# Layers 1 and 2 of a codebook convolution block: table products of units 0 and 1 issued two units sooner, and a new order of the loads ahead of the second layer

## The chip, the cores and the metric

The kernel runs on one core of one Trainium2 chip. The metric is the device time of the whole program in microseconds (us). The core has five engines, each of which executes its own queue in order: PE (matrix products; its weight loads are shown apart as PEld), DVE (vector), ACT (activations), POOL (general) and SP, which here only issues transfers. An engine whose next instruction waits for another engine lets everything behind that instruction wait too.

## The reference, cut to what matters

The input is `x`, 32 images of 1024 channels and 14 x 14 places. The first block replaces three convolutions by table look-ups with a softmax, and the second block is a linear attention, which this change does not touch.

```python
def _amm(patches, centroids, lut, inv_temp):
    ...
    v = patches.reshape(B, ncb, sub, H * W).transpose(0, 3, 1, 2)
    scores = 2.0 * jnp.einsum('blcs,cks->blck', v, centroids) - jnp.sum(centroids * centroids, -1)[None, None]
    attn = jax.nn.softmax(scores * inv_temp, axis=-1)
    out = jnp.einsum('blck,cko->blo', attn, lut)
    return out.transpose(0, 2, 1).reshape(B, -1, H, W)
...
out = _amm(x, c1_centroids, c1_lut, c1_invt)                      # layer 1
out = jax.nn.relu(_bn(out, bn1_g, bn1_b))
out = _amm(_extract3x3(out, 1), c2_centroids, c2_lut, c2_invt)    # layer 2
out = jax.nn.relu(_bn(out, bn2_g, bn2_b))
out = _amm(out, c3_centroids, c3_lut, c3_invt)                    # layer 3
out = _bn(out, bn3_g, bn3_b)
return jax.nn.relu(out + identity)
```

`_bn` normalises over the whole batch, so layer 2 can't begin before layer 1 has ended, and layer 3 not before layer 2. The input of the block is `_gn(x)`, a group normalisation for each image.

## The kernel before, in words

Four stages follow one another: layer 1, layer 2, layer 3, and the attention. Layers 1 and 2 are driven by the same function `units` (L732). The work of a layer is cut into 128 units: 16 pairs of images, and for each pair eight blocks b of 512 table rows. One unit is

- scores: small matmuls into four PSUM banks (`score1`, L903; `score2`, L1035), and four exponentials on ACT that empty them into one of six tiles `t` (L576);
- the softmax: DVE transposes `t` (L588), adds up groups of 16 (L607), inverts (L609) and transposes the inverses back (L619); POOL multiplies them onto `t` (L626), for every fourth unit with a part set aside as "spare" (L621). From unit 2 on, POOL first adds the halves of the transposed tile (L591), so DVE adds up half as much. The program's order is kept: `units` issues the transpose of unit u one turn before the rest of its softmax;
- `spare_rows` (L717): SP copies rows of the spare into `t`, one transfer or, for every fourth unit, three;
- the table product `lut(u)` (L739): 6 or 8 matmuls, recorded as 12 or 16, into two PSUM banks "po", which are held for the eight units of a pair.

Turn i of `units` issues, in this order: the scores and exponentials of unit i + 4, the transpose of unit i + 3, the softmax of an earlier unit (unit 0 in turn -3, unit 1 in turn -2, then unit 2 in turn 0, unit 3 in turn 1 and so on) with its spare rows, side work `side(i)`, and last `lut(i)` from turn 0 on.

The side work of the first turns includes the preparation of the tables, once per block b and layer, in `packed_lut` (L679): `less` subtracts the last row of each group with two matmuls and two ACT copies (L700, L701), `keep` stores a part of the table to memory (only b = 0 and 4, L704), and `others` loads it back into the block's free rows (L707). `lut(b)` needs all of it for its block. `less` writes to the "po" banks (three of them), or, for b above 5, to the "sc" banks of the scores (four of them). Layer 1 places this work by a list of turns (L857). In layer 2 the first four blocks come before `units`, and `side2` (L1054) has the others. Turns 0 to 2 of layer 1 also carry the group normalisation of the second pair: two matmuls (L274) and small DVE operations (L282 to L288).

Layer 2 reads 3 x 3 neighbourhoods. ACT writes one half (128 channels) of a pair of images into a padded tile (`store_pair`, L987), three transfers bring it to memory as `h1d`, and six transfers per unit (`load_patches`, L1005) bring the shifted rows into one of four patch tiles. All these are issued by SP, except where `engines=both` gives every second one to ACT's queue. Units 0 to 3 of a pair need half 0, units 4 to 7 half 1.

Of the kernel before, what the change touches and what calls it, by code (L numbers as in the profile page):

```python
# [149 lines left out]
def conv_preact_kernel(ctx: ExitStack, tc: tile.TileContext, a: dict, out: bass.AP):  # L150
# [356 lines left out]
    def layers(exact, early=None):  # L507
# [38 lines left out]
        def tap_row(dy, dx):  # L546
            return 8 * dx + dy if dx < 2 else 3 + dy
# [16 lines left out]
        def scores(n):  # L564
            return ps_sc.tile([P, 512], F32, tag="sc", name="sc")[:, :n]
# [7 lines left out]
        def exponentials(t, scs, bias):  # L573

            for j, sc in enumerate(scs):
                nc.scalar.activation(  # L576
                    t[:, j, : sc.shape[1]],
                    sc,
                    AF.Identity if exact else AF.Exp,
                    bias=bias[:, j : j + 1],  # L580
                )

        def token_major(pool, t, two=False, halve=False):


            tf = t.rearrange("p j n -> p (j n)")
            tt = pool.tile([P, tf.shape[1]], F32, tag="tt", name="tt", bufs=2 if two else 1)
            nc.vector.transpose(tt, tf)  # L588
            tv = tt.rearrange("p (m k) -> p m k", k=KC)
            if halve and not exact:  # L590
                nc.gpsimd.tensor_tensor(tv[:, :, :8], tv[:, :, :8], tv[:, :, 8:], ALU.add)  # L591
                tv = tv[:, :, :8]
            return tt, tv
# [85 lines left out]
        def packed_lut(layer, b):  # L679


            v = weights[b].rearrange("p (s w) -> p s w", s=4)
            kept = tables[2 * layer - 2 + b // 4].rearrange("(c k) w -> c k w", k=KC)
            j0 = 0 if b % 4 else 1
            k0 = b % 4 - 1 if b % 4 else 3

            def own():
                if layer == 1:
                    nc.sync.dma_start(v, lut1_tiles[b].rearrange("j c k w -> (c k) j w"))
                    return  # L690
                for c in range(4):
                    nc.sync.dma_start(v[32 * c : 32 * c + 32], lut2_tiles[b, c])

            def less():
                for h in range(2):
                    t = weights[b][:, 512 * h : 512 * h + 512]
                    ps = scores(512) if b > 5 else None
                    if ps is None:
                        ps = ps_po.tile([P, 512], F32, tag="po", name="less")
                    nc.tensor.matmul(ps, less_last, t, start=True, stop=True)  # L700
                    nc.scalar.copy(t, ps)  # L701

            def keep():
                nc.sync.dma_start(tables[2 * layer - 2 + b // 4], v[:, 0])  # L704

            def others():
                nc.sync.dma_start(v[15::16, j0:], kept[:, k0 : k0 + 13 - 4 * j0 : 4])  # L707

            return v, own, less, keep, others


# [20 lines left out]
        def units(ahead, ts, pool, luts, score, bias, dst, stats, side, last, halve=False):  # L732

            n = 8 * NP
            po, late, tts = [], [], {}

            def lut(u):  # L739
                p, b = divmod(u, 8)  # L740
                if b == 0:
                    po[:] = [
                        ps_po.tile([P, 512], F32, tag="po", name="po")[:, :N2] for h in range(2)
                    ]
                j0 = 0 if b % 4 else 1
                order = [(h, j) for h in range(2) for j in range(j0, 4)]
                for h, j in order if b == 7 else sorted(order, key=lambda k: k[1]):
                    nc.tensor.matmul(  # L748
                        po[h],
                        luts[b][:, j, h * P : (h + 1) * P],  # L750
                        ts[u % len(ts)][:, j, :N2],
                        start=(b == 0 and j == j0),
                        stop=(b == 7 and j == 3),
                    )
                if b == 7:
                    for h in range(2):
                        o = dst[:, h, p * N2 : (p + 1) * N2]
                        nc.scalar.copy(o, po[h])
                        late.append((stats[:, h, p, :], o))

            for i in range(-ahead, n):
                u = i + ahead
                if u < n:
                    scs = score(u)
                    exponentials(ts[u % len(ts)], scs, bias[:, 4 * (u % 8) :][:, :4])
                u = i + ahead - 1
                if 0 <= u < n:
                    tts[u] = token_major(pool, ts[u % len(ts)], halve, halve and u >= DIRECT)
                if halve and u >= DIRECT:
                    u = u - 1 if u > DIRECT else n  # L770
                if 0 <= u < n:
                    softmax(
                        pool,
                        u,
                        ts[u % len(ts)],
                        *tts.pop(u),
                        spare=spares[u // 4 % 2] if u % 4 == 0 else None,
                        steps=(1, 1, 1) if u == 0 and not exact else None,
                    )
                    spare_rows(ts, u)  # L780
                while late:
                    nc.vector.bn_stats(*late.pop(0))
                side(i)
                if i >= 0:
                    lut(i)
            for h in range(2):
                nc.vector.bn_stats(*late.pop(0))
                last(h)
# [4 lines left out]
        with ExitStack() as s:  # L793
# [11 lines left out]
            def at(i, piece):  # L805
                todo.setdefault(max(i, -AHEAD - 1), []).append(piece)
# [30 lines left out]
            def side(i):  # L837
                for f in todo.pop(i, []):
                    f()
# [10 lines left out]
            luts2 = [packed_lut(2, b) for b in range(8)]  # L850
# [3 lines left out]
                    at(8 * p + c - AHEAD - 1 - (p == 0), normalise(p, c))  # L854
            at(24, edges)
            at(40, masks2)
            for b, i in enumerate((-4, -3, -3, -2, -2, -1, -1, 0)):  # L857
                for k in (2, 3, 4):
                    if k != 3 or b % 4 == 0:
                        at(i, lambda b=b, k=k: luts[b][k]())  # L860
# [110 lines left out]
        with ExitStack() as s:  # L971
# [15 lines left out]
            def store_pair(p, h, engines=(nc.sync,)):  # L987
                t = pads[h]
                nc.scalar.activation(
                    t.rearrange("p (i r c) -> p i r c", r=15, c=15)[:, :, :14, :14],  # L990
                    out1[:, h, p * N2 : (p + 1) * N2].rearrange(
                        "p (i r c) -> p i r c", r=14, c=14
                    ),
                    AF.Relu,
                    bias=bi1[:, h : h + 1],
                    scale=sc1[:, h : h + 1],
                )
                for x in range(3):
                    c0 = LEAD + 2 * p * IMG + 1 - x
                    v = h1d[x // 2][h, :, :, c0 : c0 + 2 * IMG]  # L1000
                    engines[x % len(engines)].dma_start(v[:, x::2] if x < 2 else v, t)
# [3 lines left out]
            def load_patches(u, engines=(nc.sync,)):  # L1005
                p, b = divmod(u, 8)
                h, g = divmod(b, 4)
                for n, (src, rows) in enumerate(zip(h1d, (8, 16))):
                    for dy in range(3):
                        c0 = LEAD + 2 * p * IMG + 15 * (dy - 1)  # L1010
                        engines[dy % len(engines)].dma_start(
                            pbuf[u % NPB][tap_row(dy, 2 * n) :: rows, :, :SPAN],
                            src[h, 4 * g : 4 * g + 4, :, c0 : c0 + SPAN].rearrange(
                                "q r n -> r q n"
                            ),
                        )

            both = nc.sync, nc.scalar
            store_pair(0, 0, engines=both)
            luts2[0][2]()  # L1020
            luts2[1][2]()
            load_patches(0, engines=both)
            load_patches(1)
            luts2[0][3]()
            luts2[2][2]()
            luts2[3][2]()
            store_pair(0, 1)
            load_patches(2)
            luts2[7][1]()
            for b in range(4):  # L1030
                luts2[b][4]()
            load_patches(3)
            w9, bias2 = parts[2]

            def score2(u):  # L1035
# [16 lines left out]
            ahead = 1 if exact else 4  # L1052
# [429 lines left out]
    engines = {ENG.PE, ENG.DVE, ENG.Activation, ENG.Pool, ENG.SP}  # L1482
    pre = ctx.enter_context(ExitStack())
    early, weights4, repeated = attention_inputs(pre)
    with tc.manual_schedule(engines=engines):
        again = layers(False, early)
# [800 lines left out]
```

## Time and profile before

| | |
|---|---|
| median of three runs | 3363.78 us (3362.78 to 3363.94) |
| profiled execution, its own time | 3366.47 us |
| its span | 3364.7 us, mean granted PE clock 0.993 |
| layer 1, from its first matmul to the end of its last table product | about 10 to 828 us |
| layer 2, the same | about 838 to 1637 us |
| PE busy over the span | 98% |
| DVE, POOL, ACT busy over the span | 85%, 75%, 53% |

The busy shares are averages over four stages with different limits. The change concerns the first 100 us of layer 1 and the first 90 us of layer 2. A timeline entry reads: start, duration, engine, line, operation, output and input, number of merged instructions, and in brackets how long the engine had been idle and what ended it.

### The profile page before, as it was taken

How to read it: one execution, taken by the hardware profiler on the slowest of the kernel's cores; microseconds unless marked ns; L12 is line 12 of the kernel's file. 1: busy time of each engine (PE TensorE's matmuls, PEld its weight loads, DVE VectorE, ACT ScalarE, POOL GpSimd, SP SyncE). 2: the span in 40 equal slices, each digit the busy share in tenths (PEclk: the TensorE clock that was granted, in tenths of full speed). 3: DMA queues.
4: the chain of work that ended last, by engine and by line, in shares of the span. 5: the costliest groups of instructions: out<-in, count | busy, mean ns of one | idle time of the engine just before them, and what ended most of it. 6: DMA issues, size and time to landing. Idle time of an engine off the chain costs nothing. (4 is left out here: it accounts for less than half of the span.)

```text
span 3364.7 us, 61037 instructions
## 1 busy us (share of the span) xinstructions
PE 3300.0 (98%) x22287; PEld 2014.9 (60%) x22287; DVE 2871.1 (85%) x4174; ACT 1788.2 (53%) x4419; POOL 2528.3 (75%) x1562
## 2 busy tenths in 40 slices
PE   8999999999899999999999999998999999999999
PEld 4555555554344444454478888885666666666665
DVE  8999999997788899888656667655899999999996
ACT  4555555554444444444311111107888888888886
POOL 5999999997788888888432222215988888888888
PEclk9999999999999999999999999999999999999999
DMA  3110110102444344443231111113233333232321
GB/s 120 46 49 28 47 47 28 46 28 73 143 124 124 110 123 126 119 115 109 64 81 50 50 50 41 47 47 125 66 89 98 90 89 98 78 91 84 94 81 49
DMA packets 242253, 266.34 MB, mean 79 GB/s; under 512 B 32812, under 2 KB 239700, under 8 KB 241944
## 3 DMA queue, kind: packets, MB, share of 16 engines
q1 hardware_dynamic: 241104, 261.79, 26.6%
q8 instruction: 180, 2.95, 0.4%
q14 instruction: 129, 1.06, 0.1%
q10 hardware_dynamic: 840, 0.55, 0.1%
HBM read 171.01 MB, written 75.58 MB: 73 GB/s over the span
## 5 line engine op out<-in xcount | busy, mean ns | idle before, releaser
L626 POOL TENSOR_TENSOR t<-t,r 128x1568 f32<-128x1568 f32 (+5 forms) x292 | 962.1, 3296 | 535.3 <-issue 223.8
L748 PE MATMUL po<-t,lut 128*128 128x392 f32 x3840 | 1329.5, 499 | 5.8 <-DMA t<-spare 4.8
L748 PEld LDWEIGHTS po<-t,lut 128*128 128x128 f32 x3840 | 709.3, 190 | 602.2 <-issue 71.0
L1794 PE MATMUL mm<-y,lut 128*128 128x392 f32 x2048 | 714.6, 494 | 1.8 <-DVE k L1810 1.8
L588 DVE STREAM_TRANSPOSE tt<-t 128x1568 f32<-128x1568 f32 (+1 forms) x284 | 517.7, 1823 | 155.9 <-ACT t L576 152.8
L576 ACT ACTIVATE t<-sc,cbias 128x392 f32<-128x392 f32 (+1 forms) x624 | 322.4, 598 | 560.8 <-PE sc L909 188.4
L2018 DVE SCALAR_TENSOR_TENSOR pa<-y,lepe_w,pa 128x406 f32<-128x406 f32 x900 | 536.7, 638 | 19.3 <-PE pa L2000 17.0
L619 DVE STREAM_TRANSPOSE r<-rc 128x1568 f32<-128x1568 f32 (+1 forms) x284 | 520.8, 1834 | 11.6 <-POOL t L626 1.2
L1794 PEld LDWEIGHTS mm<-y,lut 128*128 128x128 f32 x2048 | 369.4, 188 | 243.5 <-issue 6.3
L591 POOL TENSOR_TENSOR tt<-tt 128x784 f32<-128x784 f32 x252 | 463.5, 1839 | 11.2 <-DVE tt L588 11.1
L576 ACT ACTIVATE t<-sc,room 128x392 f32<-128x392 f32 x512 | 259.1, 589 | 392.2 <-issue 162.9
L1376 PE MATMUL po<-t,lut 128*128 128x224 f32 (+2 forms) x1352 | 315.0, 416 | 0.0
L607 DVE TENSOR_REDUCE sm<-tt 128x98 f32<-128x784 f32 (+2 forms) x284 | 297.0, 1046 | 1.6 <-POOL tt L591 0.8
L1376 PEld LDWEIGHTS po<-t,lut 128*128 128x128 f32 (+1 forms) x1352 | 234.6, 190 | 63.2 <-issue 60.6
L609 DVE RECIPROCAL rc<-sm 128x98 f32<-128x98 f32 (+1 forms) x284 | 220.2, 775 | 9.8
L630 ACT ACTIVATE sm<-sm 128x98 f32<-128x98 f32 (+1 forms) x284 | 85.3, 300 | 157.0 <-DVE rc L609 157.0
L1980 POOL TENSOR_TENSOR qr<-qr,zb 128x784 f32<-128x784 f32 x64 | 118.3, 1856 | 49.4 <-DMA zb<-zd 49.2
L1647 ACT ACTIVATE w<-x,tb,gn_a 128x196 f32<-128x196 f32 x248 | 128.3, 517 | 35.9 <-POOL y L1529 28.4
L1806 ACT ACTIVATE e<-e 128x392 f32<-128x392 f32 x256 | 134.4, 525 | 1.0
L1043 PE MATMUL sc<-patch,room 27*32 27x392 f32 x4096 | 124.0, 509 | 8.6 <-DMA patch<-h1d 6.6
L1760 ACT ACTIVATE y<-x,gb,ga 128x196 f32<-128x196 f32 x256 | 123.3, 541 | 13.6 <-POOL gb L1723 13.6
L1389 DVE TENSOR_TENSOR o<-po,o 128x224 f32<-128x224 f32 (+1 forms) x156 | 81.6, 543 | 56.7 <-PE po L1376 51.9
(215 smaller groups left out, 4523.1 us busy)
## 6 DMA issues: line engine op xcount, KB each, us to landing
patch<-h1d SPq DMA_DIRECT2D x383, 108.5 KB
x<-in_x_dram SPq DMA_DIRECT2D x32, 784.0 KB
o3d<-o SPq DMA_DIRECT2D x56, 448.0 KB
x<-in_x_dram SPq DMA_DIRECT2D x64, 392.0 KB
out_dram<-x SPq DMA_DIRECT2D x64, 392.0 KB
o<-o3d SPq DMA_DIRECT2D x62, 392.0 KB
h1d<-pad SPq DMA_DIRECT2D x95, 225.0 KB
patch<-h1d SPq DMA_DIRECT2D x383, 54.2 KB
```

Of the source, the lines that this page charges most:

```text
L576: nc.scalar.activation(t[:, j, : sc.shape[1]], sc, AF.Identity if exact else AF.Exp, bias=bias[:, j : j + 1],)
L588: nc.vector.transpose(tt, tf)
L591: nc.gpsimd.tensor_tensor(tv[:, :, :8], tv[:, :, :8], tv[:, :, 8:], ALU.add)
L607: nc.vector.tensor_reduce(sm, tv, AX.X, ALU.add)
L609: nc.vector.reciprocal(rc, sm)
L619: nc.vector.transpose(r, bc(rc, 2, KC))
L626: nc.gpsimd.tensor_tensor(v[:, c], v[:, c], r[:, c], ALU.mult)
L748: nc.tensor.matmul(po[h], luts[b][:, j, h * P : (h + 1) * P], ts[u % len(ts)][:, j, :N2], start=(b == 0 and j == j0), stop=(b == 7 and j = ...
L1376: nc.tensor.matmul(dst, w, x, start=start, stop=stop)
L1794: nc.tensor.matmul(pv(), w[kt][:, m0 : m0 + P], ywin(p, first + kt), start=(kt == 0), stop=(kt == 3),)
L1806: nc.scalar.activation(e(), e(), AF.Exp, scale=-1.0)
L2018: nc.vector.scalar_tensor_tensor(acc, neighbours(p, c, offset(k)), lw[:, c, k : k + 1], acc, ALU.mult, ALU.add,)
```

## The change

The diff does five things.

1. `units`: `lut(0)` is issued at the end of turn -2 and `lut(1)` at the end of turn -1. Turns 0 and 1 issue no table product, and from turn 2 on all is as before. This holds for layers 1 and 2.
2. `less` of blocks 4 and 5 writes to the "sc" banks as well.
3. The preparation of the tables of layer 1 is spread differently: by blocks 0 to 7, turns -4, -4, -3, -3, -1, 0, 0, 1 instead of -4, -3, -3, -2, -2, -1, -1, 0.
4. The first `store_pair` of layer 2 is issued by SP alone. The patches of unit 1 are issued by SP and ACT in turn.
5. Ahead of layer 2's `units`, the patches of units 2 and 3 come before the store of half 1, the load-back of block 0 (`others`) comes between them, and the raw table of block 7 is loaded last.

```diff
@@ -694,7 +694,7 @@
-                    ps = scores(512) if b > 5 else None
+                    ps = scores(512) if b > 3 else None
...
@@ -781,8 +781,9 @@
                 side(i)
-                if i >= 0:
-                    lut(i)
+                k = {-2: 0, -1: 1, 0: -1, 1: -1}.get(i, i) if ahead > 2 else i
+                if k >= 0:
+                    lut(k)
...
@@ -854,7 +855,7 @@
-            for b, i in enumerate((-4, -3, -3, -2, -2, -1, -1, 0)):
+            for b, i in enumerate((-4, -4, -3, -3, -1, 0, 0, 1)):
                 for k in (2, 3, 4):
                     if k != 3 or b % 4 == 0:
                         at(i, lambda b=b, k=k: luts[b][k]())
...
@@ -1016,20 +1017,21 @@
             both = nc.sync, nc.scalar
-            store_pair(0, 0, engines=both)
+            store_pair(0, 0)
             luts2[0][2]()
             luts2[1][2]()
             load_patches(0, engines=both)
-            load_patches(1)
+            load_patches(1, engines=both)
             luts2[0][3]()
             luts2[2][2]()
             luts2[3][2]()
+            load_patches(2)
+            luts2[0][4]()
+            load_patches(3)
             store_pair(0, 1)
-            load_patches(2)
+            for b in range(1, 4):
+                luts2[b][4]()
             luts2[7][1]()
-            for b in range(4):
-                luts2[b][4]()
-            load_patches(3)
             w9, bias2 = parts[2]
```

Here `luts[b][1]` to `luts[b][4]` are `own` (the raw load), `less`, `keep` and `others` of block b.

## The prediction

> **What bounds the kernel now.** I read the page's slices first, then engine busy time by windows, then the timelines of the two places where the slices show gaps, and last SP's own waits.
>
> ```profile
> PE   8999999999899999999999999998999999999999
> DVE  8999999997788899888656667655899999999996
> ```
>
> A slice is 84 us. PE has a gap only at the start, where layer 1 turns into layer 2, and later where the attention begins. Windows (PE, PEld, DVE, ACT, POOL busy, then PE clock):
>
> ```profile
> 20.00:40.00 20.00, 15.62 (x49) 6.55 (x48) 16.21 (x24) 14.37 (x33) 6.66 (x8) 0.85 0.37 119
> 40.00:60.00 20.00, 20.00 (x73) 9.76 (x73) 18.76 (x30) 13.30 (x31) 16.28 (x7) 1.00 0.35 101
> 600.00:800.00 200.00, 200.00 (x776) 104.03 (x776) 188.28 (x203) 108.06 (x272) 187.95 (x84) 1.00 0.09 27
> 850.00:870.00 20.00, 14.44 (x85) 5.42 (x86) 14.56 (x11) 9.69 (x22) 13.26 (x8) 0.77 0.54 160
> ```
>
> In the steady part PE is full, and DVE and POOL are at 94%. So a delay at the start stays to the end of a layer if it is PE's. One of DVE is made good slowly, about 1.7 us per eight units. PE is idle for 4.4 us between 20 and 40 and not at all from 40 on: there is hardly a hole in which the early products could go. Layer 1's timeline:
>
> ```profile
> 33.72 2.53 SPq L728 DMA_DIRECT2D t<-spare  x3
> 40.83 0.94 PE L909 MATMUL sc<-x,cw 32*128 32x392 f32 x8
> 43.50 0.60 SPq L725 DMA_DIRECT2D t<-spare  x1
> 49.90 0.20 DVE L282 TENSOR_TENSOR gd<-gst,gn_ps 128x32 f32<-128x32 f32 x1 [0.75 <-PE gn_ps L274]
> 50.67 1.80 DVE L588 STREAM_TRANSPOSE tt<-t 128x1568 f32<-128x1568 f32 x1
> 71.03 3.52 POOL L626 TENSOR_TENSOR t<-t,r 128x1568 f32<-128x1568 f32 x1
> 79.65 5.51 PE L748 MATMUL po<-t,lut 128*128 128x392 f32 x16
> ```
>
> These are the spare rows of units 0 and 1, the scores of unit 3, DVE's wait for the group means, the transpose of unit 4, and unit 5's last multiplication and table product. Layer 2:
>
> ```profile
> 857.05 1.62 PE L1043 MATMUL sc<-patch,room 27*32 27x392 f32 x32 [4.07 <-DMA patch<-h1d]
> 858.75 1.98 SPq L728 DMA_DIRECT2D t<-spare  x3
> 876.71 0.62 SPq L725 DMA_DIRECT2D t<-spare  x1
> 879.07 5.50 PE L748 MATMUL po<-t,lut 128*128 128x392 f32 x16 [0.69 <-DMA t<-spare]
> 905.07 5.50 PE L748 MATMUL po<-t,lut 128*128 128x392 f32 x16 [1.93 <-DMA t<-spare]
> ```
>
> ```profile
> SPq L1001 <- DMA h1d<-pad: 2.4, 1, 2.4
> ```
>
> PE waits for patches, then twice for spare rows (units 2 and 6). Unit 2's were multiplied by 869.83 (POOL, 866.29 + 3.54) but issued at 876.71: SP, busy almost without a break with 0.62 us per patch transfer, is the limit there.
>
> **What the Trainium skill says.** "TensorE: Matmul & The Clock Gate", Part 1, What's actually happening: after about 3.4 us without work the clock is halved, and about 3.4 us of work bring it back. The trace agrees: after PE's pause from 853 to 857 the windows show 0.50 until 862. "DMA: Bandwidth & Descriptors", Issuing engines are not separate DMA queues: a second issuing engine saves issue time only. Here SP's third store waits 2.4 us for another store, which the split brought with it. Same page, Two DMAs through the same engine are not ordered: a dependent transfer must wait for completion. The trace prices that: 876.71 to 879.07, 2.35 us from issue to use.
>
> **Layer 1, step by step.**
> 1. Unit 0's tile is multiplied by 35.66 and its third spare transfer issues at 35.68; with 2.35 it is ready at 38.0. Turn -2 leaves PE nothing after unit 2's scores (about 34.3), so PE waits 3.7 us in front of `lut(0)`, with unit 3's scores behind it. 12 records take 4.2 us: 42.2. Such a wait can also halve the clock; then 43.9.
> 2. Unit 3's scores then go at 42.2 instead of 40.83, its exponentials end 0.96 + 2.02 later, at 45.2. DVE is free at 43.6: it stalls 1.6 us where it stalled 0.26.
> 3. `lut(1)` waits for unit 1's spare row, 43.50 + 2.35 = 45.85 (block 4's `less` fits ahead of it), and takes 5.5: 51.35. Behind it stand unit 4's scores (before: 45.33). Exponentials end at 54.3.
> 4. Behind those now stand `less` of blocks 5 and 6, in score banks that the exponentials must free first: 52.8 to 56.3 (four at 0.86). Then the group-mean matmuls, 0.7. DVE's group-norm step goes at 57.2 instead of 49.90, and with 0.8 for it unit 4's transpose at 58.0 instead of 50.67: 7.3 us late.
> 5. From there to unit 5's tile the trace shows DVE idle 0.4 us and POOL following it, so 74.55 becomes about 81.9, ready at 84.25. Unit 5's product ran at 79.65 and was ready at 74.57 + 2.35 = 76.9: slack 2.75. It starts 4.6 late, 5.9 with the halved clock. I take 5.2.
> 6. Later units have their slack (unit 12: 0.7 us, but DVE has 2 us of idle time ahead of it), so 0 to 0.5 more, taken as 0.
>
> The four `less` copies taken out of turns -2 and -1 save ACT time that only shortens its own idleness. They cost nothing early because unit 1's and 2's exponentials (30.6, 36.5) still precede DVE's need (33.5, 40.8). Bank choice costs what step 4 holds.
>
> **Layer 2.**
> 1. SP's queue. The wait of 2.4 goes, 0.45 for one more store comes, two patch issues (1.23) go to ACT, and a 0.5 wait mostly goes. The rest is reordered: I count 41 issues from 829.4 and reach unit 0's spare rows at 854.8 instead of 858.75. ACT gains two issues (0.6 to 1.4 each) ahead of the copies of blocks 2 and 3, for which block 3's `less` and the first scores wait; it loses one store issue. First scores: -0.45, bounds -1.2 to +0.5. Block 7's raw table lands before 853 and is needed past 870: nothing.
> 2. Patches of unit 3 land at about 848 instead of 857. But `lut(0)` now stands before unit 3's scores: spare rows 854.8, third issue 856.1, landed 858.4. PE has then idled since about 852.4, so half clock for its first 3.5 us: ends 864.3. Unit 3's scores go 7.2 us later than before, its transpose at 867.35 instead of 860.84.
> 3. `lut(1)` 867.5 to 873.0 (two `less` ahead of it); unit 4's scores 873.0 instead of 862.83; its transpose 876.05 instead of 866.66. So 9.4 late.
> 4. Unit 2's multiplication ends at 876.3; its spare row issues at 876.35 instead of 876.71, since SP had been late. SP now waits 4 us for it, and again for unit 3's (884.9 instead of 881.85): 3.1 late. From there SP is as full as before, and unit 6's product starts about 3.2 later than 905.07. After that PE is full. I take +3.1. At full clock in step 2 it is 1.4; with an extra ACT delay and a slower unit 5, 4.5.
>
> Both layers end in a batch norm, so the two add: 5.2 + 3.1 = +8.3. Profiled: 3366.47 + 8.3 = 3374.8. The median of the runs is 2.7 lower than the profiled time: 3363.78 + 8.3 = 3372.1. About 0.2% (6.7 us) is what a measurement can tell from no change.
>
> **Rivals.**
> - Layer 2 pays for layer 1: SP's saved 3.2 us reach unit 6's product because SP never waits for DVE. Then +5.2 - 3.2 = +2: 3366. For it: that product waits on a spare row. Against: DVE's 9.4 is larger than the 6.9 of SP's lateness at unit 2.
> - Nothing moves by more than a us or two, since slack at unit 5 swallows most: 3364. Against: 7.3 is far over 2.75.
> - Faster: DVE does not starve, because the reordered exponentials reach it in time. Its stalls of 1.4 between 40 and 67 and the 2.75 of slack go in layer 1, 3.2 in layer 2: -7.3, 3356.5. The place is unit 4's transpose in layer 1, and it decides if that starts before 50.67 + 2.75 = 53.4. For it: DVE, not PE, bounds units 2 to 5. Against: `lut(1)` can't end before 51.35.
>
> **How the numbers follow.** Both layers delayed 0.64 (its own range +4 to +12, a fifth of it under 6.7), layer 2 pays 0.15, nothing 0.07, faster 0.14. Slower 0.50, same 0.14 + 0.15 + 0.07 = 0.36, faster 0.14. Range: up to +13 (3377), down to -3 (3361), which leaves out the faster case and little else.
>
> **What would show it.** Right: in layer 1 `lut(0)` near 38 after a PE wait for a spare row, unit 4's transpose near 58, unit 5's product near 84 with a wait before it; in layer 2 unit 3's scores behind `lut(0)` near 864, and SP waiting for POOL at units 2 and 3. Wrong: unit 4's transpose before 54, or DVE without a gap between 50 and 57; or layer 2's unit 6 earlier, counted from the end of layer 1.

## The result, and the profile after

| | before | after |
|---|---|---|
| median of six runs | 3363.86 us (3362.64 to 3364.93) | 3393.95 us (3392.75 to 3396.72) |
| ratio, 95% interval | | 1.0091 (1.0078 to 1.0104) |
| profiled execution, its own time | 3366.47 us | 3393.07 us |
| its span | 3364.7 us | 3390.4 us |

The kernel is slower by 30.1 us, where the prediction had 8.3. The sign was right, the size was not. The page of the kernel after, slices (part 2) and one group (part 5, which ends in the idle time ahead of the group and what ended most of it), then the same group of before:

```profile
PE   7999999999899999999999999999999999999998
DVE  7999999997788898888666666655899999989996
...
L748 PE MATMUL po<-t,lut 128*128 128x392 f32 x3840 | 1334.5, 500 | 13.3 <-DMA t<-spare 7.4
```

```profile
L748 PE MATMUL po<-t,lut 128*128 128x392 f32 x3840 | 1329.5, 499 | 5.8 <-DMA t<-spare 4.8
```

The table products wait 13.3 us in all (before: 5.8), so they can't hold 30. PE's first slice fell from 8 to 7, as a loss in layer 1's first turns would have it, but its last slice fell too, from 9 to 8, and that lies in the attention, in which no line was changed. The span cut at four places of the trace says how much each stage took. Layer 1 ends here at the first copy that empties its last product, layer 2 at layer 3's first `less` matmul, layer 3 at the attention's first transposing matmul:

| us | layer 1 | layer 2 | layer 3 | attention |
|---|---|---|---|---|
| before | 825.5 | 811.4 | 647.7 | 1080.1 |
| after | 831.7 | 816.3 | 646.0 | 1096.5 |
| difference | +6.2 | +4.9 | -1.7 | +16.4 |

(The -1.7 is not the change's: layer 3 took either 645.7 to 646.0 or 647.4 to 647.7 in every profile of this study, though its code is the same in all.) These are two single executions: their differences add up to 25.7 us, where the medians differ by 30.1, and a stage with unchanged code repeats to within some 2 us. The two layers together lost 11.1, not far from the forecast. More than half of the loss is where the prediction had no term at all.

First the layers. Layer 1 after, timeline entries of SP, PE and DVE:

```profile
33.70 2.52 SPq L728 DMA_DIRECT2D t<-spare  x3
35.61 4.19 PE L748 MATMUL po<-t,lut 128*128 128x392 f32 x12 [1.31 <-DMA t<-spare]
45.73 7.20 PE L748 MATMUL po<-t,lut 128*128 128x392 f32 x16 [2.42 <-POOL tt L591]
52.86 0.94 PE L910 MATMUL sc<-x,cw 32*128 32x392 f32 x8
58.55 0.20 DVE L282 TENSOR_TENSOR gd<-gst,gn_ps 128x32 f32<-128x32 f32 x1 [9.66 <-PE gn_ps L274]
59.31 1.80 DVE L588 STREAM_TRANSPOSE tt<-t 128x1568 f32<-128x1568 f32 x1
64.64 1.40 PE L910 MATMUL sc<-x,cw 32*128 32x392 f32 x4 [1.41 <-ACT lut L701]
65.97 7.23 PE L748 MATMUL po<-t,lut 128*128 128x392 f32 x16
85.82 5.51 PE L748 MATMUL po<-t,lut 128*128 128x392 f32 x16
```

`lut(0)` and `lut(1)` stand at 35.61 and 45.73, each behind a wait. (The view puts the second down to POOL; it fits unit 1's spare row, issued at 43.48, as well.) Unit 4's scores come behind the second, then DVE stands still for 9.66 us in front of the group means, and unit 4's transpose starts at 59.31 instead of 50.67. The products of units 1 and 2 took 7.2 us instead of 5.5 (the granted clock was 0.83 from 40 to 50 and 0.85 from 60 to 70, where before had 1.00), and unit 5's starts 6.2 late. Layer 2 after:

```profile
862.86 1.98 SPq L728 DMA_DIRECT2D t<-spare  x3
864.95 5.88 PE L748 MATMUL po<-t,lut 128*128 128x392 f32 x12 [2.44 <-issue]
873.90 1.81 DVE L588 STREAM_TRANSPOSE tt<-t 128x1568 f32<-128x1568 f32 x1 [11.84 <-ACT t L576]
882.81 1.81 DVE L588 STREAM_TRANSPOSE tt<-t 128x1568 f32<-128x1568 f32 x1 [3.59 <-ACT t L576]
882.90 0.62 SPq L725 DMA_DIRECT2D t<-spare  x1
915.25 5.50 PE L748 MATMUL po<-t,lut 128*128 128x392 f32 x16 [2.68 <-DMA t<-spare]
```

These times hold layer 1's 6.2. Without it unit 0's spare rows are issued at 856.7, `lut(0)` starts at 858.8, the transposes of units 3 and 4 start at 867.7 and 876.6, unit 2's spare row is issued at 876.7 and unit 6's product starts at 909.1, that is 4.0 later than the 905.07 of before.

Now the attention. Windows over its whole length (busy time of PE first, then PEld, DVE, ACT, POOL), of before and of after:

```profile
2284.60:3364.70 1080.10, 1062.48 (x10102) 690.10 (x10102) 976.41 (x2062) 902.74 (x2230) 938.86 (x862) 0.99 0.30 87
```

```profile
2293.90:3390.40 1096.50, 1064.07 (x10102) 689.82 (x10102) 977.87 (x2062) 904.07 (x2230) 939.64 (x863) 0.99 0.29 86
```

The same work by the same counts of instructions (one more on POOL), but PE idles 32.4 us instead of 17.6. So the order differs. It shows best at two small DVE operations for each of the 16 pairs of images, the means `kmm` (L1926 before, L1928 after), for which the normaliser's matmuls wait. Timeline of before, for pair 2 and pair 16:

```profile
2393.42 0.18 DVE L1926 TENSOR_TENSOR kmm<-ks,hmean 128x32 f32<-128x32 f32 x1
2394.06 1.20 DVE L1926 TENSOR_TENSOR kmm<-ks,hmean 128x32 f32<-128x32 f32 x1
2415.35 1.53 PE L1944 MATMUL mm<-q,kmm 128*32 128x196 f32 x32 [0.39 <-DVE q L1810]
...
3300.68 1.82 DVE L1926 TENSOR_TENSOR kmm<-ks,hmean 128x32 f32<-128x32 f32 x2
3320.59 1.53 PE L1944 MATMUL mm<-q,kmm 128*32 128x196 f32 x32
```

And of after, with two of POOL's entries beside the last:

```profile
2401.64 0.18 DVE L1928 TENSOR_TENSOR kmm<-ks,hmean 128x32 f32<-128x32 f32 x1
2435.92 0.19 DVE L1928 TENSOR_TENSOR kmm<-ks,hmean 128x32 f32<-128x32 f32 x1
2436.76 1.51 PE L1946 MATMUL mm<-q,kmm 128*32 128x196 f32 x32
...
3350.66 1.71 POOL L1840 TENSOR_TENSOR qr<-q,cosq 128x784 f32<-128x784 f32 x1
3352.99 8.02 DVE L1928 TENSOR_TENSOR kmm<-ks,hmean 128x32 f32<-128x32 f32 x2
3358.86 7.36 POOL L2057 TENSOR_TENSOR x<-x,side 128x392 f32<-128x392 f32 x7
3363.18 1.53 PE L1946 MATMUL mm<-q,kmm 128*32 128x196 f32 x32
```

Before, the two means of pair 2 are 0.6 us apart and 22 us ahead of the normaliser. After, the second is 34 us behind the first, directly ahead of the normaliser. For the last pair both hang beside POOL's unbroken run, and the normaliser comes 1069.2 us after the start of the attention instead of 1036.0, with 27 us to the end.

Why should an untouched stage be ordered otherwise? Its order is not written out. A planner (`Plan`, L51) writes it from pieces with ranks. The lines that matter are L90 and L127:

```python
engines = {p[0] for p in self.pieces}
...
for e in engines:
    ...
    if locked and any(t > now for o, t in port.items() if o != e):
        rest.append((r, n))
        continue
```

`engines` is a set of strings. The order in which Python walks such a set is drawn anew in every build. Pieces marked `port=True` hold a lock that DVE and POOL share in the plan: nearly all of these are POOL's, and the means are DVE's only ones. Where POOL is asked first, it takes the lock again the moment it is free, and the means get in only once POOL has nothing ready. The planner's loop, run off the chip over all 120 orders of the five engines, gives just two plans, one for DVE ahead of POOL and one for POOL ahead of DVE, 60 orders each, for before and after alike. By the planner's own clock, which adds up the durations written beside the pieces, the first ends at 1084.8 us and the second at 1102.7. Theory: before was built with the first, after with the second, and the 19 us that the layers leave of the 30.1 have nothing to do with the diff. Rival: the diff reaches the attention through the state in which it leaves the engines, buffers or queues, or the layers' delay shifts it.

### The profile page after: what moved, and what is told of

It reads as the page before. It is cut to its first block, busy times and chain, and to the rows that moved or that the text cites. A ratio compares the mean times of both kernels' runs of the same rounds, so it can differ in the third digit from the quotient of the medians.

```text
span 3390.4 us, 61032 instructions
## 1 busy us (share of the span) xinstructions
PE 3303.7 (97%) x22287; PEld 2015.7 (59%) x22287; DVE 2871.6 (85%) x4174; ACT 1790.1 (53%) x4419; POOL 2528.6 (75%) x1562
## 5 line engine op out<-in xcount | busy, mean ns | idle before, releaser
L748 PE MATMUL po<-t,lut 128*128 128x392 f32 x3840 | 1334.5, 500 | 13.3 <-DMA t<-spare 7.4
L2020 DVE SCALAR_TENSOR_TENSOR pa<-y,lepe_w,pa 128x406 f32<-128x406 f32 x900 | 534.5, 638 | 22.2 <-PE pa L2002 19.9
L591 POOL TENSOR_TENSOR tt<-tt 128x784 f32<-128x784 f32 x252 | 463.4, 1839 | 29.9 <-DVE tt L588 29.8
L609 DVE RECIPROCAL rc<-sm 128x98 f32<-128x98 f32 (+1 forms) x284 | 220.2, 775 | 9.8
L630 ACT ACTIVATE sm<-sm 128x98 f32<-128x98 f32 (+1 forms) x284 | 85.1, 300 | 160.4 <-DVE rc L609 160.3
L825 ACT ACTIVATE x<-x,gn_b,gn_a 128x196 f32<-128x196 f32 x256 | 127.6, 557 | 5.1 <-POOL gn_b L296 3.4
```

What stands on the lines that cost most here:

```text
L609: nc.vector.reciprocal(rc, sm)
L748: nc.tensor.matmul(po[h], luts[b][:, j, h * P : (h + 1) * P], ts[u % len(ts)][:, j, :N2], start=(b == 0 and j == j0), stop=(b == 7 and j = ...
L2020: nc.vector.scalar_tensor_tensor(acc, neighbours(p, c, offset(k)), lw[:, c, k : k + 1], acc, ALU.mult, ALU.add,)
```

## Experiments: the attention

The runs below were made in three batches, each beside the kernel before and on the same chip as it. Its medians there were 3363.36, 3363.97 and 3364.00 us for runs 1 to 4, 5 to 8 and 9 to 12: the build with DVE first, as run 1 will show.

**1. The kernel before, with POOL first.**

```diff
-        engines = {p[0] for p in self.pieces}
+        engines = ["PE", "POOL", "ACT", "DVE", "SP"]
```

> The kernel before with one line changed: the planner of the attention goes through its engines in a written order with POOL ahead of DVE, instead of in the order of a Python set of strings. Theory 'plan' (the attention's order of instructions depends on the set's order, which the build draws anew, and the changed kernel drew the other one): the attention takes about 1096.5 us instead of 1080.1, total +16, near 3380. Rival 'carried over' (layers 1 and 2 leave something behind that slows the attention): no difference, 3364.

Measured: 3381.73 us (3379.57 to 3384.29), ratio 1.0057 (1.0044 to 1.0071), +18.4. Timeline entries of it:

```profile
2388.98 0.18 DVE L1926 TENSOR_TENSOR kmm<-ks,hmean 128x32 f32<-128x32 f32 x1
2423.28 0.19 DVE L1926 TENSOR_TENSOR kmm<-ks,hmean 128x32 f32<-128x32 f32 x1
2424.11 1.51 PE L1944 MATMUL mm<-q,kmm 128*32 128x196 f32 x32
...
3340.22 8.03 DVE L1926 TENSOR_TENSOR kmm<-ks,hmean 128x32 f32<-128x32 f32 x2
```

The same gap of 34 us and the same 8 us at the end as in after, without a line of the change.

**2. The kernel after, with DVE first** (the list `["PE", "DVE", "ACT", "POOL", "SP"]` in the same place, as in all the runs that follow but number 11).

> The changed kernel with the same line written with DVE ahead of POOL. Theory 'plan': the attention is back at 1080, total near 3363.9 + 9.4 = 3373 to 3377; what is left are about 6 us of layer 1 and 4 to 5 of layer 2. Rival 'carried over': still near 3394.

Measured: 3374.83 us (3372.73 to 3379.35), ratio 1.0037 (1.0025 to 1.0050), +11.5. 11.5 and 18.4 add up to 29.9, which is the result's 30.1 within their intervals (each some 4 us to either side). The start of the normaliser's matmuls, in us from the start of the attention, is the fingerprint:

| pair | 1 | 2 | 3 | 15 | 16 |
|---|---|---|---|---|---|
| before | 68.1 | 130.8 | 195.7 | 974.7 | 1036.0 |
| run 2, the change with DVE first | 68.1 | 130.8 | 195.7 | 974.6 | 1036.0 |
| after | 67.0 | 142.8 | 196.4 | 988.7 | 1069.2 |
| run 1, before with POOL first | 68.2 | 144.0 | 197.4 | 989.7 | 1070.3 |
| run 11 (below) | 67.6 | 131.1 | 195.3 | 982.2 | 1045.3 |

The attention follows the order of the engines in the planner, and not the change: the rival falls. (The attention as a whole took 1096.5 and 1097.5 us in after and run 1, and 1080.1 and 1080.5 in before and run 2.)

**11. POOL first, but the means don't ask for the lock.**

```diff
-                do(DVE, rank - 10, 0.2, means(i), allk, [("kmm", i)], port=True)
+                do(DVE, rank - 10, 0.2, means(i), allk, [("kmm", i)])
```

> The kernel before with GpSimd named ahead of VectorE in the planner of the attention stage, as in the run that cost 18.4 us, but with the two small means of each pair no longer asking for the shared lock. Theory A, that the lock alone makes the order matter, by holding back these means: 0 to 4 us above before. Theory B, that GpSimd's own order of pieces makes the loss: 14 to 19 us above before.

Measured: 3376.13 us (3372.62 to 3377.72), ratio 1.0034 (1.0022 to 1.0047), +12.1: between the two theories. Pair 2 is back at 131.1, and the hole ahead of the last pair is gone. With this edit the two orders of the engines give the very same instructions in the same order on every engine, so it is through the lock at the means, and only there, that the order acts. But leaving the lock out is no cure. All instructions of this tile (number, then shortest, median and longest in ns), in before and in run 11:

```profile
L1926 DVE TENSOR_TENSOR kmm<-ks,hmean x32: 175/209/1757, 2329.6 to 3300.8; 128x32 f32<-128x32 f32 x32
```

```profile
L1926 DVE TENSOR_TENSOR kmm<-ks,hmean x32: 175/828/1757, 2327.6 to 3307.0; 128x32 f32<-128x32 f32 x32
```

Planned without the lock, the means run beside POOL's operations and last four times as long in the median. The Trainium skill has a reason ("SBUF — State Buffer", SBUF: two separate sides): a DVE operation with two SBUF inputs and a GpSimd (POOL) operation that reads SBUF need the same port pair, which one takes for a whole instruction while the other is blocked. The trace agrees as to these means: 0.18 us alone, 8.0 us for two beside POOL's run in after. DVE's busy time in the attention is 986.3 us here against 976.4 in before. How the 12 us split between such blocking and the other plan that comes of it was not settled; the planner's own clock, which leaves blocking out, ends this plan at 1083.1 us, no later than before's.

## Experiments: the two layers

**3 and 4. Each layer's share alone.** The turn of `lut` and the banks made to depend on the layer; run 3 has layer 1's new products, banks and spread and layer 2 as before, run 4 the reverse (with the new loads).

```diff
-                k = {-2: 0, -1: 1, 0: -1, 1: -1}.get(i, i) if ahead > 2 else i
+                k = {-2: 0, -1: 1, 0: -1, 1: -1}.get(i, i) if ahead > 2 and soon else i
```

> DVE ahead of POOL in the planner; layer 1 as changed (products sooner, weights later, blocks 4 and 5 in score banks), layer 2 as before. My theory (DVE starved by the early products): +6.2 over the kernel before, unit 5's product of layer 1 near 85.8. Rival (the two layers' costs do not add, a late layer 1 is made good later): under +3.

> DVE ahead of POOL in the planner; layer 2 as changed (products sooner, new order of loads), layer 1 as before. My theory: +4 to +5 over the kernel before, unit 6's product of layer 2 about 4 later, counted from the end of layer 1. Rival (the loads pay for the products): 0 or below.

Measured: layer 1 alone 3370.15 (3366.99 to 3375.05), ratio 1.0019 (1.0012 to 1.0027), +6.8; layer 2 alone 3369.19 (3364.33 to 3372.86), ratio 1.0015 (1.0008 to 1.0022), +5.8. Their sum, 12.6, is run 2's 11.5 within the intervals: they do add. The traces agree. Layer 1, counted from its first scores because these start anywhere from 19.9 to 22.1 us, took 809.5 to 809.9 us in the three traces with all of its change (after, runs 2 and 3), and 803.3 to 803.8 in the eight with its old code. Layer 2 took 814.9 to 818.6 where it was changed (after, runs 2, 4 and 8), and 809.3 to 811.4 in the five with its old code. Run 3's trace has unit 5's product at 85.5, run 4's has unit 6's 83.7 us behind the end of layer 1 (before 79.6, after 83.6).

**12. Everything but the two products**, which stay in turns 0 and 1 in both layers (the line of runs 3 and 4, with `soon` never set).

> The whole change with VectorE named first, except that the table products of units 0 and 1 keep their old place in both layers. Theory A, that their sooner place makes the layers' loss: what is left is the later table preparation of layer 1 (1.9 us measured alone) and the new loads (1.0 us the other way), so 0 to 3 us above before. Theory B, that the table preparation and the score banks lent to unit 4's and 5's tables carry half of it: 5 us or more above before.

Measured: 3365.67 (3362.51 to 3372.30), ratio 1.0006 (0.9997 to 1.0014), +1.7. By the medians some 10 of run 2's 11.5 go with the place of these two products, but the interval of 1.7 alone reaches from -1 to +5, and the trace says so for layer 2 only. Layer 2 took 809.7 there, as with its old code. Layer 1, counted from its first scores, took 807.5: still 3.7 to 4.2 more than the old code, with the products in their old place. PE and DVE in turns -1 and 0:

```profile
39.38 2.93 PE L700 MATMUL sc<-lut,less_last 128*128 128x512 f32 x3 [2.45 <-ACT t L576]
45.44 5.36 PE L700 MATMUL sc<-lut,less_last 128*128 128x512 f32 x8
51.19 0.20 DVE L282 TENSOR_TENSOR gd<-gst,gn_ps 128x32 f32<-128x32 f32 x1 [2.69 <-PE gn_ps L274]
```

PE waits 2.45 us for score banks in front of block 4's weight difference, works at half clock behind that (0.50 from 40 to 48, where before had 1.00), and DVE waits 2.69 for the group means. So, by this one trace, the table preparation and its banks delay layer 1 by themselves, and only some 2 of its 6 us go with the products. How far the parts depend on each other was not settled: no run has layer 1's new products with the old spread and banks.

**7. Layer 1's spread of the table preparation alone.**

```diff
-            for b, i in enumerate((-4, -3, -3, -2, -2, -1, -1, 0)):
+            for b, i in enumerate((-4, -4, -3, -3, -1, 0, 0, 1)):
```

> The kernel before (DVE ahead of POOL) with only the new turns of the table preparation of layer 1, and the products where they were. My theory (the early products are what costs): within 1.5 of the kernel before. Rival (blocks 5 and 6 moved in front of the group means are what costs): +3 or more.

Measured: 3365.86 (3361.40 to 3372.52), ratio 1.0007 (1.0001 to 1.0014), +1.9. A small cost, between the theories; in the trace layer 1, from its first scores, is 2.1 to 2.6 longer than with the old code (805.9). Its timeline shows where:

```profile
48.59 5.05 PE L748 MATMUL po<-t,lut 128*128 128x392 f32 x10 [2.07 <-ACT lut L701]
...
57.54 0.17 DVE L288 TENSOR_SCALAR gve<-gn_ps 128x16 f32<-128x16 f32 x1 [3.03 <-PE gn_ps L274]
```

Within unit 0's product PE now waits 2.07 us for ACT's copies of a weight difference that is made in the same turn, in the "po" banks that the product needs. DVE waits 3.03 for the second group mean, which stands on PE behind the next block's weight difference.

**8. The change with DVE first, and the first two group-mean steps one turn sooner**, so that they stand ahead of `lut(1)`.

```diff
-(-3, -3, -2, -1, 0, 0, 1, 1, 2)[k]
+(-3, -3, -2, -1, -1, 0, 1, 1, 2)[k]
```

> The changed kernel (DVE ahead of POOL) with one piece moved: the group-mean matmuls of layer 1 are issued a turn sooner, ahead of the product of unit 1. My step 4 (3.4 us of DVE's stall are the wait for these matmuls behind four weight matmuls, the rest is unit 4's exponentials): DVE's transpose of unit 4 near 55.9 instead of 59.3, total 3.4 below the changed kernel with this planner order, near 3371.5. Rival (PE itself, not DVE, sets the end of the ramp): unchanged, 3375.

Measured: 3371.82 (3371.26 to 3375.11), ratio 1.0026 (1.0014 to 1.0037): 3.0 below run 2, near the 3.4 of the forecast. The two intervals overlap; in the traces layer 1 from its first scores is 2.3 shorter than in run 2 (807.2 and 809.5).

```profile
48.66 0.15 DVE L282 TENSOR_TENSOR gd<-gst,gn_ps 128x32 f32<-128x32 f32 x1
...
55.73 1.81 DVE L588 STREAM_TRANSPOSE tt<-t 128x1568 f32<-128x1568 f32 x1 [6.27 <-ACT t L576]
...
63.93 5.53 PE L748 MATMUL po<-t,lut 128*128 128x392 f32 x16
```

The group means are done at 48.66, and unit 4's transpose, 3.6 sooner than in after, now waits for its exponentials. PE's pause of 1.41 us ahead of unit 2's product is gone, and that product runs in 5.53 us instead of 7.23. Layer 1 is still 3.4 to 3.9 longer than with the old code, which this run does not divide between the products and the table preparation.

**5 and 6. Layer 2's new loads alone, and its products alone** (with the old loads).

> The kernel before (DVE ahead of POOL in the planner) with only the new order of the loads and stores ahead of layer 2; all products where they were. My theory (SP's queue is the limit at unit 6 of layer 2, and the new order shortens it): unit 0's spare rows issued 3 to 4 us sooner, unit 6's product 2 to 4 us sooner, total -2 to -4. Rival (another wait takes its place at once): 0 within 1.

> The kernel before (DVE ahead of POOL) with only the products of units 0 and 1 of layer 2 issued sooner and the bank choice for that layer; the loads in their old order. My theory (the products block unit 3's and 4's scores until late spare rows come): worse than with the new loads, +7 to +10 over the kernel before, since unit 0's spare rows land 4 us later. Rival (the new loads are what costs): +2 or less.

Measured: loads alone 3362.97 (3358.75 to 3366.18), ratio 0.9996 (0.9987 to 1.0004), not told from no change; products alone 3369.65 (3368.00 to 3372.67), ratio 1.0019 (1.0010 to 1.0027), +5.7, the same as with the new loads. Both medians missed what I expected: the loads are worth nothing that can be told here (layer 2 took 810.6 us in run 5's trace, as with its old code). Run 5's timeline says why:

```profile
864.48 4.11 PE L748 MATMUL po<-t,lut 128*128 128x392 f32 x12
...
867.05 8.90 SPq L1011 DMA_DIRECT2D patch<-h1d  x12
876.05 0.62 SPq L725 DMA_DIRECT2D t<-spare  x1
878.38 6.91 PE L748 MATMUL po<-t,lut 128*128 128x392 f32 x16 [2.58 <-DMA t<-spare]
```

In before that product stood at 867.06, so it starts 2.6 sooner (2.1 counted from the end of layer 1). But unit 2's waits 2.58 us for spare rows that stand behind twelve patch issues in SP's queue, and starts where it did (879.07), at a lower clock.

**9. The kernel before, with each turn's patches asked for behind its spare rows** instead of ahead of its scores, and **10, the same with the new loads.**

```diff
             def score2(u):
-                if 0 < u and u + NPB - 1 < 8 * NP:
-                    load_patches(u + NPB - 1)
...
             def side2(i):
+                u = i + ahead
+                if 0 < u and u + NPB - 1 < 8 * NP:
+                    load_patches(u + NPB - 1)
```

> The kernel before (VectorE named first), with one move: in layer 2 the patches of the unit three ahead are asked for behind the spare rows of the same turn, not ahead of the scores. Theory A, that SyncE's queue of patch issues holds up spare rows and with them the products of unit 2 (0.7 us of waiting) and unit 6 (1.9 us): both waits go, and the kernel is 1.5 to 3 us faster than before. Theory B, that these waits only take up slack that the next unit's exponentials would impose anyway: within 1 us of before.

> The move of the run before it, together with the change's order of the first patch loads of layer 2. Theory A, that the loads' gain of about 2 us at units 0 and 1 was lost only to unit 2's spare rows behind twelve patch issues: now it survives to the end of the layer, 3 to 4.5 us faster than before. Theory B, that the exponentials set the pace behind unit 2: 1 to 2 us faster at the most, as with the move alone.

Measured: run 9 3361.61 (3358.07 to 3364.57), ratio 0.9991 (0.9983 to 1.0000), -2.4; run 10 3363.74 (3358.73 to 3367.89), ratio 1.0000 (0.9991 to 1.0008), -0.3. Run 9, units 2 and 6:

```profile
871.84 0.62 SPq L725 DMA_DIRECT2D t<-spare  x1
876.92 5.53 PE L748 MATMUL po<-t,lut 128*128 128x392 f32 x16
...
897.81 0.61 SPq L725 DMA_DIRECT2D t<-spare  x1
900.95 5.53 PE L748 MATMUL po<-t,lut 128*128 128x392 f32 x16
```

Both waits of before (0.69 and 1.93) are gone, but a gain is not shown: the interval ends at 1.0, layer 2 took 810.1 us in the trace, where the old code took 809.3 to 811.4, and unit 6's product came 77.7 us behind the end of layer 1, which run 1's trace has at 77.5 with the old code. Run 10 has neither wait either, and unit 6's product at 77.4. So patches that come sooner bought nothing that can be told here, even with SP's queue out of the way. The gain of 3 to 4.5 that I expected of run 10 isn't there; its interval (-3 to +3 us) holds the 1 to 2 of the other theory as well as nothing, and overlaps run 9's.

## Why the prediction was wrong

**The step that failed** is the sum: "Both layers end in a batch norm, so the two add: 5.2 + 3.1 = +8.3." It has two terms, and there was a third, +18.4 (run 1), from the stage that nobody touched. The prediction put that term at nothing without saying so: I took the attention as fixed because the diff leaves it alone. Its order is made at build time by a planner whose loop runs over a set, and the kernel after was a build in which POOL came ahead of DVE. Nothing in the profile of before could tell which way that would fall, but L90 was there to be read, and the planner's own clock, 17.9 us apart for the two orders, gives the size. So a second case, some 18 us higher, could have stood beside every other in the range.

**Layer 1.**
- Step 1 put `lut(0)` at 38.0, behind the third spare transfer. It started at 35.61, before the third was even fully issued (33.70 + 2.52 = 36.2): its first matmuls need the first transfer alone. No cost came of it.
- Step 3 put `lut(1)` at 45.85 (45.73), with 5.5 us to its end. It took 7.2, at the lower clock that the windows show after PE's wait of 2.42; step 1 had such a fall in mind for `lut(0)`.
- Step 4: group-norm step 57.2 (58.55), transpose of unit 4 at 58.0 (59.31). The 1.3 is the rest of the slower product. Run 8 shows this link to be real.
- Step 5: unit 5's product at 84.25 to 85.6 (85.82), but by another way than the one I gave. From unit 2's product at 65.97 PE goes on without a wait; the wait ahead of unit 5 that I had named as a sign isn't there. So it isn't unit 5's tile that ends last, but PE's own lost time: the pauses ahead of `lut(0)`, `lut(1)` and unit 2, and two products at the lower clock with 1.7 us more each. From the first scores to unit 5's product PE idled 8.2 us instead of 4.4 and was busy 2.4 us longer. DVE's delay does reach PE, but at unit 2 and through ACT: the pause of 1.41 is a wait for ACT's copies, which stood in ACT's queue behind its sum for an earlier unit (L630), and that waited 1.44 us for DVE's inverses (L609).
- "They cost nothing early", said of the moved `less` copies, held: the transposes of units 1 and 2 start at 33.53 and 40.75 as before (33.54, 40.76). But their later place costs by itself: without the early products layer 1 was still 3.7 to 4.2 longer (run 12's trace), and the prediction had it only as a part of step 4, behind `lut(1)`.
- The term of 5.2 was 6.2 in the trace, 6.8 in run 3.

**Layer 2.** The chain stands as written. With layer 1's 6.2 taken off, measured against forecast: `lut(0)` 858.8 and 858.4, transposes of units 3 and 4 867.7 and 867.35, 876.6 and 876.05, unit 6's product 4.0 and 3.2 late. Only step 1's start was off, 856.7 for unit 0's spare rows instead of 854.8. The term of 3.1 was 4.0 at unit 6, 4.9 over the stage, and 5.8 in run 4; the traces of layer 2 with old and new code are 3.5 to 9.3 apart.

**The rivals.** "Layer 2 pays for layer 1" rested on SP's saving reaching unit 6; run 5 shows that saving to be lost at unit 2. "Nothing moves" needed unit 5's slack of 2.75 to swallow the delay; its product was 6.2 late. "Faster" needed unit 4's transpose before 53.4; it came at 59.31.

So the mechanism was right in layer 2. In layer 1 it was right as far as unit 4's transpose; from there the delay reached PE by another way, and the table preparation has a larger share of it than the prediction said, so that its 5.2 came near the 6.2 in part by luck. Together 8.3 was 11.5 (8.4 to 16.8, run 2); what made the prediction wrong by another 18.4 was no part of the change.

## What to carry to other kernels

Cut the trace by stages before explaining a difference, and look at the stages that the diff leaves alone: where an order is drawn at build time, two builds of one source need not be one program. Where a planner or a loop runs over a set, write the order out, or a lucky draw gets credited to one change and an unlucky one charged to another. And in a ramp, work that is issued early on a queue that runs in order takes its wait along: a product that waits for its inputs holds back the scores that feed all later units.

## What the hardware showed that I had not expected

- Two DVE operations of 0.18 us each lasted 8.0 us together (after; 8.03 in run 1), one of them 7.9 alone, while POOL worked through its queue without a break in instructions of 1.0 to 1.7 us. DVE was held over a row of POOL's instructions, not over a single one. That it was the port which held it is the Trainium skill's reason and was not shown apart.
- PE ran its next product at a lower clock after pauses shorter than one product: 7.20 us instead of 5.5 after a pause of 2.42 (after), 6.91 after 2.58 (run 5), 7.23 after one of 1.41 with a few scores between; where run 8 took that last pause away, the same product took 5.53. But the length of the pause alone does not decide: after 2.68 us ahead of unit 6 in layer 2 (after), and after 1.93 at the same place in before, the product took 5.50. What decides was not settled.
